# A selective scan whose delta products share TensorE's rows, whose sums are split in two, and whose transposed input is stored once

## The chip, the core and the metric

The kernel runs on one core of a Trainium2 chip. The core has TensorE (PE in the profile; its weight loads are PEld), VectorE (DVE), ScalarE (ACT), GpSimd (POOL) and SyncE (SP), which issues nearly all DMAs of this kernel. Each engine works through its own queue in order and waits on semaphores. The metric is the device time of one execution in microseconds.

## The reference

Four layers follow each other on a tensor of 2 x 128 x 128 pixels with 128 channels, each as `x = x + layer(groupnorm(x))`: window attention, a Fourier layer with a feed-forward part, a recurrence in the Fourier domain, and a selective scan (layer 3). Only layer 3 is touched. Cut to what matters:

```
xc = silu(depthwise_conv3x3(x @ W_in[:, :256]))             # 256 channels
xs = [rows, columns, rows reversed, columns reversed]       # four orders of the pixels, within 4 x 4 blocks of 32 x 32
for k in range(4):
    dt(8), B(16), C(16) = split(x_proj_w[k] @ xs[k])         # per pixel
    delta = softplus(dt_proj_w[k] @ dt + dt_proj_b[k])       # 256 x pixels
    h[d, n] = exp(delta * A[d, n]) * h[d, n] + delta * xs[k][d] * B[n]    # scan over 16384 pixels
    y[k][d] = sum_n h[d, n] * C[n] + D[d] * xs[k][d]
out = (layernorm(sum of the y[k] put back in place) * silu(z)) @ W_out
```

All arithmetic is float32. TensorE works a float32 product off in two passes, which the trace shows as two instructions.

## The kernel before

`layer3_conv` makes `xc` and stores it twice: `xs` (channels on partitions, in two orders of pixels: rows and columns) and `xst` (pixels on partitions, 256 channels each, also in both orders). For one of the 32 blocks (`b`, `hg`, `wg`) it transposes the block on TensorE into `xt`, and SP writes it to `xst[0]` with one DMA (L1242) and to `xst[1]`, in column order, with four DMAs (L1245).

`layer3_scan` has 256 **parts**: 2 images x 4 orders k x 32 stretches of 512 pixels. k = 0 and 1 go forward, k = 2 and 3 backward. A part has 8 **slots**: slot s works on four of the 16 states of one half e of the channels (qq = s // 2, e = s % 2), as four scans over 128 x 512 elements. What one slot needs is made by five engines:

- ACT: `exponentials` (L1517, four activations into `da`), `diagonals` (L1538; small diagonal matrices `dg` with B, 8 or 4 copies in turn), and `kept` (L1601, the last states of the scans);
- PE: two units of `products` (L1567; `ups`, 64 passes each, one unit for each two scans, in two PSUM buffers);
- DVE: four scans (L1589), two after each unit of products;
- POOL: `weighted` (L1608, `hs` times C, one instruction for all four scans of a slot), and in every second slot a fourth of the `dg` tiles (L1532);
- PE: `sums` (L1550, 8 passes, which add the weighted states to `yps`).

The loop over slots g writes the engines' queues by hand (`in_order` keeps each engine to the order of the program). One turn g is: the step "head" of the table `steps`; `exponentials(g + 1)`; `kept(g - 1)`; `diagonals(g + 5)`; `weighted(g - 1)`; `tiles(g)`, which is products of half 0, scan 0, steps "0", scan 1, steps "1", products of half 1, scan 2, steps "2", scan 3, steps "3"; then `sums(g - 2)`; then the steps "end". So `kept(g - 1)` and `weighted(g - 1)` run while slot g is scanned, and the sums of slot g - 2 stand in PE's queue between the second products of slot g and the first of slot g + 1.

The table `steps` places the work that comes once a part (slot numbers within the part; the work is for the next part where it makes inputs, for the part before where it takes results):

- slot 7: `project` e = 0 (L1342) before the second products, e = 1 after them, into the PSUM tile `xdps`;
- slot 0: `projected` (ACT copies `xdps` to `xd`: 8 rows dt, 16 rows B, 16 rows C), then `turn_b` on PE (L1360);
- slot 1: `turned_b` on DVE (L1367, `bt`) behind scan 0; `ranks(0)` on PE (L1374, `dtps`) before the second products and `ranks(1)` after them; behind scan 3 `skip(0)` on DVE (L1444 or L1449), which reads `yps` of e = 0;
- slot 2: `softplus` (ACT L1385, with two loads of activation tables), `spread` (DMAs), and `skip(1)` behind scan 3;
- slot 4: `turn` (L1410, both before the second products); slot 5: `turned` (DVE L1422, `du`, behind scans 0 and 1), and in backward parts `unturn` on PE (L1473, both after the second products); slot 6: in backward parts `store` (ACT L1483) at the head, and `load_u` (L1333, `ut`; in the part from 10000.36 it is issued at 10031.92 us and read at 10073.41 us) at the end.

The tiles of `xdps`, `btps`, `dtps`, `dltps` and `ytps` share two PSUM buffers (tag "misc") in turn: `dtps` of e = 0 takes the buffer of `xdps`, `dtps` of e = 1 that of `btps`, which `turned_b` frees. `yps` has one buffer for each e.

`ranks` takes 65 rows of `xd`: rows 0 to 7 are dt, row 64 is all ones for the bias, and the rows of `dtw` between are zero.

Of the kernel before, what the change touches and what calls it, by code (L numbers as in the profile page):

```python
# [9 lines left out]
F32 = mybir.dt.float32  # L10
# [1109 lines left out]
def layer3_conv(tc, cs, ins, x3, xs, xst, sc, sh):  # L1120
# [11 lines left out]
    with ExitStack() as ctx:  # L1132
# [20 lines left out]
        for b in range(NB):  # L1153
            for hg in range(4):
# [62 lines left out]
                for wg in range(4):  # L1217
                    t = f"{b}_{hg}_{wg}"
                    xv = two.tile([P, 2, 32, 32], F32, name=f"xv_{t}", tag="xv")
                    for e in range(2):  # L1220
                        nc.scalar.copy(xv[:, e], xw[e][:, wg].rearrange("p h w -> p w h"))
                        nc.sync.dma_start(
                            xs[0, b, hg, wg, :, e, :], xw[e][:, wg].rearrange("p h w -> p (h w)")
                        )
                        nc.sync.dma_start(
                            xs[1, b, hg, wg, :, e, :], xv[:, e].rearrange("p w h -> p (w h)")
                        )
                    xt = two.tile([P, 8, 256], F32, name=f"xt_{t}", tag="xt")
                    for g in range(4):
                        tps = ps_t.tile([P, 2, 2, P], F32, name=f"xtps_{t}_{g}", tag="x3t")  # L1230
                        for j in range(2):
                            for e in range(2):
                                h0 = 4 * (2 * g + j)
                                nc.tensor.transpose(
                                    tps[:, j, e, :],
                                    xw[e][:, wg, h0 : h0 + 4, :].rearrange("p h w -> p (h w)"),
                                    cs.ident,
                                )
                        nc.scalar.copy(
                            xt[:, 2 * g : 2 * g + 2, :], tps.rearrange("p j e d -> p j (e d)")  # L1240
                        )
                    nc.sync.dma_start(xst[0, b, hg, wg].rearrange("(t p) d -> p t d", p=P), xt)  # L1242
                    cols = xst[1, b, hg, wg].rearrange("(w t h) d -> h w t d", t=8, h=4)
                    for h in range(4):
                        nc.sync.dma_start(cols[h], xt[32 * h : 32 * h + 32])  # L1245


def layer3_scan(tc, cs, ins, xs, xst, yc, ys):
# [9 lines left out]


    nc = tc.nc  # L1260
    NS, DR, NX, T = 16, 8, 40, 512
    with ExitStack() as ctx:
        pool = lambda name, bufs, **kw: ctx.enter_context(tc.tile_pool(name=name, bufs=bufs, **kw))
        w = pool("l3b_w", 1)
# [8 lines left out]
        sel = w.tile([P, 64], F32, name="sel")  # L1273
        nc.sync.dma_start(sel, ins["c_sel64"])
        xpw = w.tile([P, 4, 2, NX], F32, name="xpw")
        for k in range(4):
            nc.sync.dma_start(xpw[:, k], ins["x_projT"][k].rearrange("(e p) c -> p e c", p=P))

        dtw = w.tile([65, 4, 256], F32, name="dtw")
        nc.sync.dma_start(dtw, ins["dt_ext"])  # L1280
        xds = []
        for i in range(2):
            t = w.tile([65, T], F32, name=f"xd{i}")
            nc.gpsimd.memset(t, 0.0)
            nc.gpsimd.memset(t[64:65, :], 1.0)
            xds.append(t)

        dsk = w.tile([P, 2, 2, 2], F32, name="dsk")
# [22 lines left out]
        def tag_of(i):  # L1311
            return "_".join(map(str, parts[i]))
# [5 lines left out]
        def steps_of(rows, tb):  # L1318
            return rows.rearrange("p (j t) -> p t j", t=4)[:, tb]
# [8 lines left out]
        def load_u(i):  # L1328
            b, k, s, sub = parts[i]
            _, (hg, wg) = place(i)  # L1330
            ut = one.tile([P, 4, 256], F32, name=f"ut_{tag_of(i)}", tag="ut")
            px = xst[k % 2, b, hg, wg]
            nc.sync.dma_start(ut, px.rearrange("(s p m) d -> s p m d", s=2, m=4)[sub])  # L1333
            held[i]["ut"] = ut

        def project(e):
# [11 lines left out]
        def projected(i):  # L1348
            v = held[i]
            xd = xds[i % 2]  # L1350
            nc.scalar.copy(xd[0:NX, :], v["xps"][0:NX, :])
            v["cd"] = dr.tile([NS, T], F32, name=f"cd_{tag_of(i)}", tag="cd")
            nc.sync.dma_start(v["cd"], xd[DR + NS : NX, :])
            v["xd"] = xd

        def turn_b(i):
            v = held[i]
            v["bps"] = ps_m.tile([P, 4, NX], F32, name=f"btps_{tag_of(i)}", tag="misc")
            for j in range(4):
                nc.tensor.transpose(  # L1360
                    v["bps"][:, j, :], steps_of(v["xd"][0:NX, :], j), cs.ident[0:NX, 0:NX]
                )

        def turned_b(i):
            v = held[i]
            v["bt"] = two.tile([P, 4, NX], F32, name=f"bt_{tag_of(i)}", tag="bt")
            nc.vector.tensor_copy(v["bt"], v["bps"])  # L1367

        def ranks(e):
            def f(i):  # L1370
                k = parts[i][1]
                v = held[i]
                ps = ps_m.tile([P, T], F32, name=f"dtps_{tag_of(i)}_{e}", tag="misc")
                nc.tensor.matmul(  # L1374
                    ps, dtw[:, k, e * P : (e + 1) * P], v["xd"], start=True, stop=True
                )
                v.setdefault("dps", []).append(ps)
            return f


        def softplus(i):
            v = held[i]
            dl = one.tile([P, 2, T], F32, name=f"dl_{tag_of(i)}", tag="dl")
            for e in range(2):
                nc.scalar.activation(dl[:, e, :], v["dps"][e], AF.Softplus)  # L1385
            v["dl"] = dl

        def spread(i):
# [88 lines left out]
        def store(i):  # L1477
# [23 lines left out]
        def at(g, place):  # L1501
            for r, where, step in steps:
                i, rest = divmod(g - r, 8)
                if where == place and rest == 0 and 0 <= i < len(parts):
                    step(i)
# [31 lines left out]
                    for n in range(4):  # L1537
                        nc.scalar.activation(dg[:, n, :], sel, AF.Copy, scale=bt[:, n : n + 1])  # L1538

        def sums(g):  # L1540
            i, s, qq, e = slot_of(g)
            v = held[i]
            if qq == 0:
                v.setdefault("yps", {})[e] = ps_y.tile(
                    [P, T], F32, name=f"yps_{tag_of(i)}_{e}", tag=f"yps{e}"
                )
            hs = v.pop(("hs", s))
            for q in range(2):
                for h in range(2):
                    nc.tensor.matmul(  # L1550
                        v["yps"][e][64 * h : 64 * h + 64, :], sel, hs[:, 2 * h + q, :],
                        start=(qq == 0 and q == 0), stop=(qq == 3 and q == 1),
                    )

        def products(g, half):
            i, s, qq, e = slot_of(g)
# [17 lines left out]
        def tiles(g):  # L1574
            i, s, _, _ = slot_of(g)
            b, k, _, _ = parts[i]
            rev = k >= 2
            v = held[i]
            state = states[(b, k)]
            da = v.pop(("da", s))  # L1580
            hs = four.tile([P, 4, T], F32, name=f"hs_{tag_of(i)}_{s}", tag="hs")
            for half in range(2):
                ups = products(g, half)
                for q in range(2):
                    j = 2 * half + q
# [3 lines left out]
                    nc.vector.tensor_tensor_scan(  # L1589
                        o, a, u, state[:, 4 * s + j : 4 * s + j + 1], ALU.mult, ALU.add  # L1590
                    )
                    at(g, j)
            v[("hs", s)] = hs

        def kept(g):
# [17 lines left out]
        with in_order(tc):  # L1613
            for g in range(-13, slots + 7):
                at(g, "head")
                if 0 <= g + 1 < slots:
                    exponentials(g + 1)
                if 0 <= g - 1 < slots:
                    kept(g - 1)
                if 0 <= g + 5 < slots:  # L1620
                    diagonals(g + 5)
                if 0 <= g - 1 < slots:
                    weighted(g - 1)
                if 0 <= g < slots:
# [124 lines left out]
def program(tc, ins, out):  # L1749
    nc = tc.nc  # L1750
    with ExitStack() as ctx:
# [7 lines left out]
        xst = dram.tile([2, NB, 4, 4, 1024, 256], F32, name="xst")  # L1759
# [102 lines left out]
```

## Time and profile before

| | |
|---|---|
| time, median of 3 runs | 18188.72 us (18179.59 to 18199.93) |
| the profiled execution, time / span | 18196.57 us / 18194.8 us |
| mean granted clock of TensorE | 0.95 |
| PE / DVE / ACT / POOL busy | 85% / 82% / 71% / 57% of the span |
| scan stage: first and last scan start | 6328.7 us, 17676.3 us: 256 parts of 44.3 us on average |
| scans, L1589 | 8192, mean 1260 ns, busy 9831.4 us; idle before them 963.1 us |
| weighted, L1608 | 2048, mean 4549 ns |
| products, L1567 | 131072 passes, busy 4488.2 us |
| sums, L1550 | 16384 passes, mean 635 ns, busy 4408.7 us |
| ranks, L1374 | 1024 passes, mean 646 ns, busy 577.7 us |
| column copies of xst, L1245 | 128 DMAs of 256 KB, 582 / 1474 / 2526 ns (least, median, most) on SP |

"Busy" is the time in which at least one instruction of the group runs, so passes that run side by side count once. "Idle before" is the engine's idle time ahead of the group, with the engine and line whose semaphore ended it. PE's instructions overlap by about 0.1 us at their ends. "issue" as the cause of a PEld gap means that no wait of the profile ended it.

### The profile page before, as it was taken

The numbers are of one execution on the slowest core, as the hardware profiler recorded it, in microseconds if no ns is written. First come the engines' busy times: TensorE is split into PE (matmuls) and PEld (weight loads), VectorE is DVE, ScalarE is ACT, GpSimd is POOL, SyncE is SP. The second block draws the span as 40 slices with busy tenths as digits, with TensorE's granted clock in tenths as the row PEclk, the third lists the DMA queues.
The fourth block names the chain that finished last, engine by engine and source line by source line (L and its number), as shares of the span: only waits on it lengthen the run. The fifth ranks groups of instructions, "written<-read, shape, count | busy, mean of one in ns | idle before, by whom it ended". The sixth has DMA issues, their size and how long they took to land.

```text
span 18194.8 us, 466190 instructions
## 1 busy us (share of the span) xinstructions
PE 15391.5 (85%) x196098; PEld 8884.8 (49%) x196098; DVE 14937.3 (82%) x18937; ACT 12999.8 (71%) x29537; POOL 10298.8 (57%) x3930
## 2 busy tenths in 40 slices
PE   7888888888666688888888888888888888888888
PEld 5555555674223344444444444444444444444445
DVE  5766666335997699999899998999999999999986
ACT  4665666333554588888888888888888888888874
POOL 0000000011000088888888888888888888888871
PEclk9999999889888799999999999999999999999999
DMA  2000000121124644444444444444444444444446
GB/s 45 23 24 23 17 17 17 57 72 54 51 57 155 207 107 116 108 118 120 119 115 108 113 117 119 120 112 114 108 113 120 123 117 108 112 112 120 118 127 192
DMA packets 1085881, 1770.68 MB, mean 97 GB/s; under 512 B 108494, under 2 KB 476878, under 8 KB 1081487
## 3 DMA queue, kind: packets, MB, share of 16 engines
q1 hardware_dynamic: 1009918, 1716.69, 35.6%
q8 instruction: 1552, 25.43, 0.6%
q10 hardware_dynamic: 73872, 24.16, 0.5%
q14 instruction: 539, 4.41, 0.1%
HBM read 1128.22 MB, written 343.93 MB: 81 GB/s over the span
## 4 chain that ended last, share of the span: by engine, by line
DVE 25%; ACT 22%; PE 19%; issue 4%; DMA 3%; SPq 1%; POOL 1%; DVEq 0%; ACTq 0%; POOLq 0%
DVE hs L1589 17%; ACT da L1517 9%; PE yps L1550 7%; PE ups L1567 6%; ACT dg L1538 5%; PE xdps L1342 2%; ACT L1385 2%; DVE du L1422 2%; ACT L1517 2%; ACT dl L1385 2%; DVE acc L1208 1%; DMA xc<-xs 1%; DMA cb<-cd 1%; POOL hs L1608 1%; ACT states L1601 1%
## 5 line engine op out<-in xcount | busy, mean ns | idle before, releaser
L1589 DVE TENSOR_TENSOR_SCAN hs<-da,states,ups 128x512 f32<-128x512 f32 x8192 | 9831.4, 1260 | 963.1 <-PE ups L1567 652.9
L1608 POOL TENSOR_TENSOR hs<-hs,cb 128x2048 f32<-128x2048 f32 x2048 | 9295.4, 4549 | 1516.5 <-ACT states L1601 1194.8
L1517 ACT ACTIVATE da<-db,na 128x512 f32<-128x512 f32 x8192 | 5224.3, 710 | 3.1
L1567 PEld LDWEIGHTS ups<-dg,du 64*64 64x64 f32 x131072 | 3611.4, 133 | 3081.9 <-issue 2811.0
L1567 PE MATMUL ups<-dg,du 64*64 64x128 f32 x131072 | 4488.2, 276 | 710.4 <-DVE hs L1589 612.7
L1550 PE MATMUL yps<-hs,sel 128*64 128x512 f32 x16384 | 4408.7, 635 | 378.7 <-POOL hs L1608 375.2
L1538 ACT ACTIVATE dg<-sel,bt 128x64 f32<-128x64 f32 x12288 | 3152.1, 335 | 0.3 <-PE ups L1567 0.2
L1550 PEld LDWEIGHTS yps<-hs,sel 128*64 128x64 f32 x16384 | 1114.1, 141 | 2268.7 <-issue 1787.4
L386 PE MATMUL tps<-ident,s 128*128 128x128 f32 x8192 | 1230.6, 288 | 434.8 <-DVE pT L389 270.2
L391 ACT COPY pT<-tps 128x512 f32<-128x512 f32 x1280 | 722.9, 584 | 1118.9 <-PE tps L386 1118.6
L306 POOL TENSOR_TENSOR xres<-xres,rowb 128x256 f32<-128x256 f32 x128 | 94.2, 737 | 2449.6 <-DMA xres<-in_x 1831.9
L358 DVE CUSTOM_DVE_ANT_1 s<-sps,relbias 128x512 f32<-128x512 f32 x2048 | 1321.0, 682 | 139.8 <-PE sps L341 134.4
L386 PEld LDWEIGHTS tps<-ident,s 128*128 128x128 f32 x8192 | 902.5, 144 | 1029.9 <-issue 499.5
L1601 ACT COPY states<-hs 128x4 f32<-128x4 f32 x2048 | 386.3, 189 | 1407.1 <-DVE hs L1589 1406.8
L371 ACT ACTIVATE s<-s,nm 128x1024 f32<-128x1024 f32 x1024 | 1163.7, 1138 | 130.3 <-DVE nm L369 127.5
L1156 POOL MEMSET xpad<- 128x34 f32 x8 | 1.3, 162 | 1153.0 <-PE xs L1030 1104.7
L1532 POOL TENSOR_TENSOR dg<-sel,bt 128x256 f32<-128x256 f32 x1024 | 633.1, 618 | 7.5 <-DVE bt L1367 7.5
L341 PE MATMUL sps<-kc,qT 32*128 32x512 f32 x4096 | 620.9, 675 | 1.9 <-DVE qT L326 1.2
L1342 PE MATMUL xdps<-xc,xpw 128*40 128x512 f32 x1024 | 541.7, 611 | 43.4 <-DMA xpw<-in_x_projT 26.1
L1374 PE MATMUL dtps<-xd,dtw 65*128 65x512 f32 x1024 | 577.7, 646 | 0.3 <-DVE bt L1367 0.2
L389 DVE COPY pT<-tps 128x512 f32<-128x512 f32 x768 | 527.6, 687 | 57.7 <-PE tps L386 55.9
L404 PE MATMUL ops<-pT,v 128*32 128x128 f32 x16384 | 500.3, 274 | 0.0
(283 smaller groups left out, 14782.3 us busy)
## 6 DMA issues: line engine op xcount, KB each, us to landing
cb<-cd SPq DMA_DIRECT2D x512, 1024.0 KB
db<-dl SPq DMA_DIRECT2D x1024, 256.0 KB
xc<-xs SPq DMA_DIRECT2D x256, 512.0 KB
ut<-xst SPq DMA_DIRECT2D x256, 512.0 KB
yc<-ysb SPq DMA_DIRECT2D x128, 512.0 KB
yf<-yc SPq DMA_DIRECT2D x128, 512.0 KB
ys<-yt SPq DMA_DIRECT2D x128, 512.0 KB
y<-ys SPq DMA_DIRECT2D x128, 512.0 KB
```

The costliest lines, as they stand in the source:

```text
L358: nc.vector.tensor_tensor_reduce(blocks(v["s", qt][:, h, 512 * g : 512 * g + 512]), blocks(v["sps", qt, g][h]), bias[:, h, :, r0 : r0 + WS ...
L371: nc.scalar.activation(s[:, h, :], s[:, h, :], AF.Exp, bias=nm[:, 2, h : h + 1], scale=-1.0, accum_out=v["sums"][:, qt, h : h + 1],)
L386: nc.tensor.transpose(tps[:, j, :], v["s", qt][:, h, k0 : k0 + P], cs.ident)
L391: nc.scalar.copy(dst, tps)
L1342: nc.tensor.matmul(v["xps"][0:NX, :], xpw[:, k, e, :], v["xc"][:, e, :], start=(e == 0), stop=(e == 1),)
L1385: nc.scalar.activation(dl[:, e, :], v["dps"][e], AF.Softplus)
L1517: nc.scalar.activation(da[:, j, :], held[i]["db"][:, e, j // 2, :], AF.Exp, scale=na[:, k, c : c + 1])
L1538: nc.scalar.activation(dg[:, n, :], sel, AF.Copy, scale=bt[:, n : n + 1])
L1550: nc.tensor.matmul(v["yps"][e][64 * h : 64 * h + 64, :], sel, hs[:, 2 * h + q, :], start=(qq == 0 and q == 0), stop=(qq == 3 and q == 1),)
L1567: nc.tensor.matmul(out[64 * n : 64 * n + 64, r, tb], v["du"][64 * r : 64 * r + 64, tb, 64 * row : 64 * row + 64], dg[:, :, n, :], start=Tr ...
L1589: nc.vector.tensor_tensor_scan(o, a, u, state[:, 4 * s + j : 4 * s + j + 1], ALU.mult, ALU.add)
L1608: nc.gpsimd.tensor_tensor(hs, hs, cb.unsqueeze(1).to_broadcast([P, 2, 2 * T]), ALU.mult)
```

## The change

Three edits, all in layer 3:

1. **One copy of `xst`.** `layer3_conv` writes each block once, in row order. `load_u` reads the column orders (k odd) from it with eight DMAs instead of one, each for every eighth partition, in runs of 1 KB where they were 4 KB.
2. **`ranks` in two row groups.** `x_proj` gets zero columns and a second copy of dt, so that `xd` has 56 rows: dt in rows 0 to 7 and again in 32 to 39, B in 8 to 23, C in 40 to 55. The product of e = 0 uses rows 0 to 31, that of e = 1 rows 32 to 63, and both are issued one after the other in slot 1, before the second products. The bias goes into the softplus activation. `xpw`, `dtw` and the new `dtb` are loaded with 12, 2 and 1 DMAs instead of 4 and 1, after two memsets.
3. **`sums` in two halves.** The four passes of q = 0 of `sums(g - 2)` stand behind the first products of slot g (and the steps "0" and "1"), those of q = 1 behind the second products (and the steps "2" and "3").

```diff
-                    nc.sync.dma_start(xst[0, b, hg, wg].rearrange("(t p) d -> p t d", p=P), xt)
-                    cols = xst[1, b, hg, wg].rearrange("(w t h) d -> h w t d", t=8, h=4)
-                    for h in range(4):
-                        nc.sync.dma_start(cols[h], xt[32 * h : 32 * h + 32])
+                    nc.sync.dma_start(xst[b, hg, wg].rearrange("(t p) d -> p t d", p=P), xt)
...
-    NS, DR, NX, T = 16, 8, 40, 512
+    NS, DR, NX, T = 16, 8, 56, 512
...
+        nc.gpsimd.memset(xpw, 0.0)
         for k in range(4):
-            nc.sync.dma_start(xpw[:, k], ins["x_projT"][k].rearrange("(e p) c -> p e c", p=P))
+            xp = ins["x_projT"][k].rearrange("(e p) c -> p e c", p=P)
+            for to, of, n in ((0, 0, DR + NS), (32, 0, DR), (32 + DR, DR + NS, NS)):
+                nc.sync.dma_start(xpw[:, k, :, to : to + n], xp[:, :, of : of + n])
...
-            px = xst[k % 2, b, hg, wg]
-            nc.sync.dma_start(ut, px.rearrange("(s p m) d -> s p m d", s=2, m=4)[sub])
+            px = xst[b, hg, wg]
+            if k % 2:
+                cols = px.rearrange("(h m s c) d -> s h c m d", h=8, m=4, s=2)[sub]
+                for h in range(8):
+                    nc.sync.dma_start(ut[h::8], cols[h])
+            else:
+                nc.sync.dma_start(ut, px.rearrange("(s p m) d -> s p m d", s=2, m=4)[sub])
...
-        def ranks(e):
-            def f(i):
...
-                ps = ps_m.tile([P, T], F32, name=f"dtps_{tag_of(i)}_{e}", tag="misc")
-                nc.tensor.matmul(
-                    ps, dtw[:, k, e * P : (e + 1) * P], v["xd"], start=True, stop=True
-                )
...
+        def ranks(i):
+            k = parts[i][1]
+            v = held[i]
+            v["dps"] = [
+                ps_m.tile([P, T], F32, name=f"dtps_{tag_of(i)}_{e}", tag="misc") for e in range(2)
+            ]
+            for e in range(2):
+                rows = slice(32 * e, 32 * e + 32)
+                nc.tensor.matmul(v["dps"][e], dtw[rows, k, :], v["xd"][rows, :], start=True, stop=True)
...
-                nc.scalar.activation(dl[:, e, :], v["dps"][e], AF.Softplus)
+                nc.scalar.activation(
+                    dl[:, e, :], v["dps"][e], AF.Softplus, bias=dtb[:, k, e : e + 1]
+                )
...
-            (-8, 1, turn_b), (-7, 0, turned_b), (-7, 1, ranks(0)), (-7, 2, ranks(1)),
+            (-8, 1, turn_b), (-7, 0, turned_b), (-7, 1, ranks),
...
-        def sums(g):
+        def sums(g, q):
...
-            hs = v.pop(("hs", s))
-            for q in range(2):
-                for h in range(2):
-                    nc.tensor.matmul(
-                        v["yps"][e][64 * h : 64 * h + 64, :], sel, hs[:, 2 * h + q, :],
-                        start=(qq == 0 and q == 0), stop=(qq == 3 and q == 1),
-                    )
+            hs = v[("hs", s)]
+            for h in range(2):
+                nc.tensor.matmul(
+                    v["yps"][e][64 * h : 64 * h + 64, :], sel, hs[:, 2 * h + q, :],
+                    start=(qq == 0 and q == 0), stop=(qq == 3 and q == 1),
+                )
...
                     at(g, j)
+                if g >= 2:
+                    sums(g - 2, half)
...
-                if 0 <= g - 2 < slots:
-                    sums(g - 2)
```

`turn_b` and `turned_b` move 32 rows instead of 40; the copy of `xdps` to `xd` moves 56 rows instead of 40.

More of the change, by code (lines that the diff above doesn't have):

```diff
@@ L1275, in layer3_scan @@
         xpw = w.tile([P, 4, 2, NX], F32, name="xpw")
+        nc.gpsimd.memset(xpw, 0.0)
         for k in range(4):
-            nc.sync.dma_start(xpw[:, k], ins["x_projT"][k].rearrange("(e p) c -> p e c", p=P))
-        dtw = w.tile([65, 4, 256], F32, name="dtw")
-        nc.sync.dma_start(dtw, ins["dt_ext"])
+            xp = ins["x_projT"][k].rearrange("(e p) c -> p e c", p=P)
+            for to, of, n in ((0, 0, DR + NS), (32, 0, DR), (32 + DR, DR + NS, NS)):
+                nc.sync.dma_start(xpw[:, k, :, to : to + n], xp[:, :, of : of + n])
+        dtw = w.tile([64, 4, P], F32, name="dtw")
+        nc.gpsimd.memset(dtw, 0.0)
+        for e in range(2):
+            nc.sync.dma_start(
+                dtw[32 * e : 32 * e + DR], ins["dt_ext"][0:DR, :, e * P : e * P + P]
+            )
+        dtb = w.tile([P, 4, 2], F32, name="dtb")
+        ext = ins["dt_ext"]
+        nc.sync.dma_start(dtb, bass.AP(ext.tensor, ext.offset + 64 * 1024, [[1, P], [256, 4], [P, 2]]))
         xds = []
         for i in range(2):
-            t = w.tile([65, T], F32, name=f"xd{i}")
+            t = w.tile([64, T], F32, name=f"xd{i}")
             nc.gpsimd.memset(t, 0.0)
-            nc.gpsimd.memset(t[64:65, :], 1.0)
             xds.append(t)
@@ L1352, in projected @@
             v["cd"] = dr.tile([NS, T], F32, name=f"cd_{tag_of(i)}", tag="cd")
-            nc.sync.dma_start(v["cd"], xd[DR + NS : NX, :])
+            nc.sync.dma_start(v["cd"], xd[32 + DR : NX, :])
             v["xd"] = xd
@@ L1357, in turn_b @@
             v = held[i]
-            v["bps"] = ps_m.tile([P, 4, NX], F32, name=f"btps_{tag_of(i)}", tag="misc")
+            v["bps"] = ps_m.tile([P, 4, 32], F32, name=f"btps_{tag_of(i)}", tag="misc")
             for j in range(4):
                 nc.tensor.transpose(
-                    v["bps"][:, j, :], steps_of(v["xd"][0:NX, :], j), cs.ident[0:NX, 0:NX]
+                    v["bps"][:, j, :], steps_of(v["xd"][0:32, :], j), cs.ident[0:32, 0:32]
                 )
@@ L1365, in turned_b @@
             v = held[i]
-            v["bt"] = two.tile([P, 4, NX], F32, name=f"bt_{tag_of(i)}", tag="bt")
+            v["bt"] = two.tile([P, 4, 32], F32, name=f"bt_{tag_of(i)}", tag="bt")
             nc.vector.tensor_copy(v["bt"], v["bps"])
-        def ranks(e):
-            def f(i):
-                k = parts[i][1]
-                v = held[i]
-                ps = ps_m.tile([P, T], F32, name=f"dtps_{tag_of(i)}_{e}", tag="misc")
-                nc.tensor.matmul(
-                    ps, dtw[:, k, e * P : (e + 1) * P], v["xd"], start=True, stop=True
-                )
-                v.setdefault("dps", []).append(ps)
-            return f
+        def ranks(i):
[4 more added lines that the diff above has]
+            ]
+            for e in range(2):
+                rows = slice(32 * e, 32 * e + 32)
+                nc.tensor.matmul(v["dps"][e], dtw[rows, k, :], v["xd"][rows, :], start=True, stop=True)
         def softplus(i):
             v = held[i]
+            k = parts[i][1]
             dl = one.tile([P, 2, T], F32, name=f"dl_{tag_of(i)}", tag="dl")
             for e in range(2):
-                nc.scalar.activation(dl[:, e, :], v["dps"][e], AF.Softplus)
+                nc.scalar.activation(
+                    dl[:, e, :], v["dps"][e], AF.Softplus, bias=dtb[:, k, e : e + 1]
+                )
             v["dl"] = dl
@@ L1538, in diagonals @@
                         nc.scalar.activation(dg[:, n, :], sel, AF.Copy, scale=bt[:, n : n + 1])
-        def sums(g):
+        def sums(g, q):
             i, s, qq, e = slot_of(g)
             v = held[i]
-            if qq == 0:
+            if qq == 0 and q == 0:
                 v.setdefault("yps", {})[e] = ps_y.tile(
@@ L1546, in sums @@
                 )
-            hs = v.pop(("hs", s))
-            for q in range(2):
-                for h in range(2):
-                    nc.tensor.matmul(
-                        v["yps"][e][64 * h : 64 * h + 64, :], sel, hs[:, 2 * h + q, :],
-                        start=(qq == 0 and q == 0), stop=(qq == 3 and q == 1),
-                    )
+            hs = v[("hs", s)]
[3 more added lines that the diff above has]
+                    start=(qq == 0 and q == 0), stop=(qq == 3 and q == 1),
+                )
+            if q == 1:
+                del v[("hs", s)]
         def products(g, half):
@@ L1628, in layer3_scan @@
                         at(g, j)
-                if 0 <= g - 2 < slots:
-                    sums(g - 2)
+                    for q in range(2):
+                        if 0 <= g - 2 < slots:
+                            sums(g - 2, q)
                 at(g, "end")
@@ L1758, in program @@
         xs = dram.tile([2, NB, 4, 4, P, 2, 1024], F32, name="xs")
-        xst = dram.tile([2, NB, 4, 4, 1024, 256], F32, name="xst")
+        xst = dram.tile([NB, 4, 4, 1024, 256], F32, name="xst")
         yc = dram.tile([NB, 2, 16, 2, P, 2, 512], F32, name="yc")
```

## The prediction

> **What bounds the kernel now.** I read the busy time by stage first, then the waits of the scan stage, then the timelines of one part, last the chain through the convolution stage.
>
> ```profile
> core 0: us, PE busy (x) PEld busy (x) DVE busy (x) ACT busy (x) POOL busy (x), PEclk, DMA share, GB/s
> 5629.00:6284.00 655.00, 443.44 (x1308) 216.19 (x1306) 457.59 (x380) 340.19 (x398) 4.17 (x37) 0.83 0.68 217
> 9500.00:10500.00 1000.00, 883.58 (x13662) 477.78 (x13656) 932.67 (x850) 839.36 (x2130) 881.73 (x277) 0.97 0.44 110
> ```
>
> The second row is a piece of the scan stage (11,349 us of 18,195): DVE 93%, but PE, POOL and ACT 84 to 88%. No engine is free, and buffers are short, so the order of the queues decides. The first row is `layer3_conv`: no engine above 70%, DMA 0.68.
>
> ```profile
> POOL hs L1608 <- ACT states L1601: 1194.8, 694, 32.1
> DVE hs L1589 <- PE ups L1567: 652.9, 822, 22.3
> PE yps L1550 <- POOL hs L1608: 372.5, 291, 2.4
> ```
>
> DVE loses most to products that come late (653 us), and PE loses time in front of sums, because POOL has not finished weighting. Below, P is a unit of products, S a slot's sums, W a `weighted`, and (1,0) means slot 1, half 0. I count t from the first scan of the part at 10045.96 us; the next part's is at 10088.27, so it takes 42.31 us. PE in slots 1 and 3, then DVE:
>
> ```profile
> 10049.23 1.10 PE L1567 MATMUL ups<-dg,du 64*64 64x128 f32 x32
> 10050.26 1.12 PE L1374 MATMUL dtps<-xd,dtw 65*128 65x512 f32 x2
> 10051.32 1.10 PE L1567 MATMUL ups<-dg,du 64*64 64x128 f32 x32
> 10052.35 1.12 PE L1374 MATMUL dtps<-xd,dtw 65*128 65x512 f32 x2
> 10053.41 1.94 PE L1550 MATMUL yps<-hs,sel 128*64 128x512 f32 x8
> 10055.27 1.98 PE L1567 MATMUL ups<-dg,du 64*64 64x128 f32 x64
> ...
> 10061.48 1.10 PE L1567 MATMUL ups<-dg,du 64*64 64x128 f32 x32 [1.24 <-DVE hs L1589]
> 10063.98 1.94 PE L1550 MATMUL yps<-hs,sel 128*64 128x512 f32 x8 [1.39 <-POOL hs L1608]
> ```
> ```profile
> 10051.84 0.30 DVE L1367 COPY bt<-btps 128x160 f32<-128x160 f32 x1
> 10052.06 3.62 DVE L1589 TENSOR_TENSOR_SCAN hs<-da,states,ups 128x512 f32<-128x512 f32 x3
> 10055.59 0.72 DVE L1444 SCALAR_TENSOR_TENSOR ysb<-xc,dsk,yps 128x512 f32<-128x512 f32 x1
> 10056.54 4.79 DVE L1589 TENSOR_TENSOR_SCAN hs<-da,states,ups 128x512 f32<-128x512 f32 x4 [0.23 <-PE ups L1567]
> ```
>
> From these starts: a P holds PE 1.04, `ranks` of one e 1.06, S 1.87 (half an S: 0.93 and a second change of shape, 1.01); scans follow each other every 1.17; from the start of P to its first scan 1.27; PE starts 0.15 after the scan that frees `ups`. Note that P(1,1) at 10051.32 goes *before* `ranks(1)`, which needs `bt`'s buffer, free only at 10052.14; and that P(3,1) goes before the S that waits for POOL.
>
> **Part by part: the queue of PE in the scan stage.** I replay one forward part in the new order with these durations.
>
> Slot 0: P(0,0), `turn_b`, half S, P(0,1): P(0,1) starts at 1.38 instead of 0.36, its scans at 2.65 instead of 2.37. First scan of slot 1: 4.99 (4.71).
>
> Slot 1: `bt` ends at 6.46. The product of e = 0 has its buffer; that of e = 1 waits for `bt`, now in front of everything else: queued behind it are half S, P(1,1), half S, P(2,0). It starts at 6.52. How long do two row groups take?
>
> ```profile
> 804.68 1.14 PE L341 MATMUL sps<-kc,qT 32*128 32x512 f32 x8
> ```
>
> Four products of the same shape in layer 0, eight passes in 1.14 us: they do run side by side, so `ranks` would cost 1.06 once instead of twice. But the wait decides: `ranks` ends at 7.58, half S at 8.59, P(1,1) feeds scan 2 at 9.86. DVE would be ready at 7.55: it stands 2.3 us. First scan of slot 2: 12.84, before 10.58. The 1.06 us that PE saves lies inside this wait and is worth nothing here.
>
> Slots 2 and 3: half S of the next part's slot 0 must wait for `skip` to read `yps` (12.92), which was no matter before; it ends at 13.99 and P(2,1) is in time. ACT's softplus and exponentials end as before, so W of slot 1 ends at 18.34 (17.96 before, 10063.92). The half S that waits for it stands in front of P(3,1): scan 2 of slot 3 at 20.69, 0.1 late. Slot 4 starts at 23.03, before at 21.16: of 2.3 + 0.3 us lost, the old waits ahead of slots 2 and 4 (0.23 and 0.44) absorb 0.7.
>
> Slots 4 to 7: W of slot 2 ends at 22.88, `turn` holds PE to 23.67, half S to 24.68: scans late by 0.55. Slots 5 and 6: none. Slot 7: 0.24 behind W of slot 5 (39.16). Behind the second `project` the last half S is only 1.0 long, so P of the next part feeds its scan at 44.42; before, the stall there was 0.69, now 0.58. The part takes **44.42 us, 2.11 more**. The same replay of the old order gives each scan of this part within 0.1 us. A backward part has `unturn`; its first P of slot 6 comes sooner (stall 2.1 us now, 0.66 then), but `store` delays `kept`, W of slot 5 ends at 40.45 and scan 2 of slot 7 stands 0.87: 45.70 against 43.6, again 2.1. Times 256: **+540 us**.
>
> **The clock.** Not all parts take 42.3 or 43.6 us. By the first scans of all parts, forward ones average 43.88 and backward ones 44.81; undisturbed ones are 1.57 and 1.21 faster. The reason, in the part before:
>
> ```profile
> 10015.20:10018.60 3.40, 1.32 (x34) 1.09 (x36) 3.40 (x4) 3.40 (x12) 3.40 (x2) 0.99 0.99 221
> 10018.60:10022.00 3.40, 3.40 (x12) 0.61 (x12) 2.49 (x3) 3.40 (x10) 3.40 (x1) 0.50 1.08 249
> ```
>
> When PE is busy for less than about 1.6 us of a stretch of 3.4 us, its granted clock is 0.50 in the next: the sums there take 3.56 us instead of 1.94. The old order makes two gaps side by side in slot 3 (1.24 and 1.39 above). In the replay the longest gaps are about 1.6 (slot 1), 1.3 and 1.3 (slots 2 and 3), each alone within 3.4 us, so PE stays at 1.8 us or more. I let a third of the excess remain: 1.39 x 256 x 2/3 = **-237 us**; bounds 0 and -356.
>
> [...]
>
> **One copy of xst.** Between two groups of rows the chain through `layer3_conv` is SP and DMA; some of its pieces:
>
> ```profile
> 5795.99 1.40 SPq L1245
> 5797.43 1.95 SPq L1245
> 5799.42 6.03 DMA xst<-xt
> 5805.55 1.08 ACT xt L1239 x2
> ```
>
> On the chain from 5620 to 6340 us L1245 has 11.0%, 79 us, and the transfers of xst 6.2%, 45 us. Both can go, but ACT's copies (25 us in each 61 us gap of DVE) stand behind them. I take **-75**, bounds -40 and -110. In the scan, seven more issues in 128 parts, 0.3 to 0.6 us each on SP (rows of L1333 and L1397), with `ut` issued 41 us before its use and SP idle between: nothing; without that cover, 4 us x 128 = 512. The start of the stage issues 10 more loads of about 0.46 us ahead of `na`, which is on the chain: **+5**. The softplus bias and the narrower `bt` (0.30 to about 0.25): nothing.
>
> **Sum.** 18,196.6 + 540 - 237 - 75 + 5 = 18,430. The profiled execution is 8 us above the median, so 18,422.
>
> **Rivals.**
> - *The clock stays as disturbed as before* (the gaps fall together after all): 18,196.6 + 540 - 75 + 5 - 8 = 18,659. For it: PE's total idle time hardly changes. Against: the replay spreads it.
> - *No half-clock stretch is left, and the convolution gains its most*: 540 - 356 - 110 + 5, so 18,268. For it: no replayed stretch is under 1.8 us.
> - *The products do not run side by side* (the second pass of e = 0 also waits behind `bt` and the second product comes after it): 1.06 more in slot 1, nothing behind it to absorb it: +271, 18,693. Against: the row of L341.
> - *Faster:* P of the next slot stands behind a half S instead of a whole one, so DVE's waits for `ups` shrink. At most all 653 us go, with 75 of the convolution 17,461; half of them, 17,790. It decides if W ends before P(g,0) is done and `bt` is ready when PE reaches `ranks`. The third row of waits and the replay speak against both: PE reaches `ranks` at 4.5, `bt` ends at 6.5.
>
> **How the numbers follow.** Forecast 0.52; clock as before 0.16; no half clock 0.14; not side by side 0.08; faster 0.10. The replay is off by perhaps 0.4 us a part, 100 us. A measurement tells 0.2%, 36 us, from no change; the case without half clock comes that near in about a third. Faster 0.10, same 0.05, slower 0.85. The range goes from the third case less part of that error, 18,230, to the fourth, 18,700.
>
> **What would show it.** DVE's wait for `ups` grows, mostly ahead of scan 2 of slot 1 (about 2.3 us, 256 times), and PE waits about 1.6 us for `bt` in L1374. The busy time of L1374's successor halves. PE waits for POOL oftener, and half-clock stretches become rare. The column issues are gone from the chain of `layer3_conv`, and the first scan starts about 70 us earlier. I am wrong if scan 2 of slot 1 does not wait, or if parts get shorter than 43.6 us.

## The result, and the profile after

| | before | after |
|---|---|---|
| median of 4 runs | 18185.44 us | 18518.22 us |
| ratio, with its 95% interval | | 1.0181 [1.0164, 1.0199] |
| the profiled execution, time / span | 18196.57 / 18194.8 us | 18519.72 / 18517.9 us |
| first scan, last scan start | 6328.7, 17676.3 us | 6168.9, 17996.5 us |
| scan stage between them | 11347.5 us | 11827.6 us |
| an undisturbed forward / backward part | 42.31 / 43.61 us | 44.50 / 45.72 us |
| mean forward / backward part | 43.88 / 44.81 us | 45.64 / 46.83 us |
| starts of a half-clock stretch in the scan stage | 168 | 162 |

("Undisturbed" is the 5th percentile of the parts, taken from the first scans of all 256.) The change makes the kernel 1.8% slower. The 323 us between the two profiled executions are a first scan that comes 160 us earlier, a scan stage that takes 480 us more, and 3 us elsewhere.

The busy time by stage in after: a piece of `layer3_conv` that ends 45 us ahead of the first scan, as the row of before did, and the same piece of the scan stage.

```profile
5629.00:6124.00 495.00, 424.73 (x1316) 198.04 (x1314) 458.88 (x383) 339.99 (x403) 4.16 (x37) 0.95 0.62 224
9500.00:10500.00 1000.00, 880.15 (x13048) 443.06 (x13048) 897.80 (x810) 809.19 (x2032) 841.00 (x262) 0.97 0.44 106
```

The convolution does the same work (DVE 459 us, ACT 340 us) in 495 us instead of 655, and its granted clock is 0.95 instead of 0.83. In the scan stage DVE goes from 93% to 90% and POOL from 88% to 84%, at the same clock of 0.97: the engines wait more, for each other.

The waits of after:

```profile
POOL hs L1624 <- ACT states L1617: 1281.9, 664, 38.9
DVE hs L1603 <- PE ups L1581: 1065.0, 1317, 25.8
PE yps L1562 <- POOL hs L1624: 408.2, 635, 3.2
PE dtps L1388 <- DVE bt L1378: 255.0, 255, 1.5
```

DVE's wait for products grew from 653 to 1065 us, PE's waits for weighted states came 635 times instead of 291, and the last line is new: once a part, PE waits for `bt`. PE in slots 1 to 3 of an undisturbed part (its first scan is at 10043.21 us), then DVE in slot 1:

```profile
10047.66 1.12 PE L1388 MATMUL dtps<-xd,dtw 32*128 32x512 f32 x2
10049.77 1.09 PE L1388 MATMUL dtps<-xd,dtw 32*128 32x512 f32 x2 [0.99 <-DVE bt L1378]
10050.79 1.08 PE L1562 MATMUL yps<-hs,sel 128*64 128x512 f32 x4
10051.80 1.10 PE L1581 MATMUL ups<-dg,du 64*64 64x128 f32 x32
...
10056.28 1.08 PE L1562 MATMUL yps<-hs,sel 128*64 128x512 f32 x4 [1.33 <-DVE ysb L1457]
...
10061.77 1.08 PE L1562 MATMUL yps<-hs,sel 128*64 128x512 f32 x4 [1.33 <-POOL hs L1624]
10062.78 1.10 PE L1581 MATMUL ups<-dg,du 64*64 64x128 f32 x32
```
```profile
10049.36 0.26 DVE L1378 COPY bt<-btps 128x128 f32<-128x128 f32 x1
10053.04 2.45 DVE L1603 TENSOR_TENSOR_SCAN hs<-da,states,ups 128x512 f32<-128x512 f32 x2 [2.23 <-ACT dl L1396]
```

The first line is the product of e = 0, both passes; the second is that of e = 1, 2.1 us later, behind `bt`. The two don't run side by side. Behind them stand a half S and P(1,1), and DVE waits 2.23 us for scan 2 of slot 1. The profile names ACT's softplus there, which ended 0.03 us before the scan began; but P(1,1), which the scan reads, had started 1.24 us before it, about the usual distance (1.27 in the part of before). Further down, the half S of slot 1 waits for POOL in front of P(3,1).

Fold all parts: ahead of scan 2 of slot 1 DVE stands 3.04 us on average in forward parts (3.16 in backward ones), and 0.5 us ahead of scan 2 of slot 4. And 159 of the 162 starts of a half-clock stretch now lie in slot 1, where before had none (there they lay in slots 3 and 5 or 6).

### The profile page after: what moved, and what is told of

Same layout as the page of the kernel before. It is cut to its first block, busy times and chain, and to the rows that moved or that the text cites. A ratio compares the mean times of both kernels' runs of the same rounds, so it can differ in the third digit from the quotient of the medians.

```text
span 18517.9 us, 467052 instructions
## 1 busy us (share of the span) xinstructions
PE 15768.0 (85%) x196098; PEld 8713.8 (47%) x196098; DVE 15016.5 (81%) x18937; ACT 13109.7 (71%) x29538; POOL 10305.6 (56%) x3930
## 4 chain that ended last, share of the span: by engine, by line
DVE 29%; PE 28%; ACT 11%; issue 5%; DMA 2%; POOL 1%; SPq 1%; DVEq 0%; POOLq 0%; ACTq 0%
DVE hs L1603 21%; PE ups L1581 11%; PE yps L1562 10%; ACT dg L1551 3%; ACT da L1530 3%; PE dltps L1423 1%; PE xdps L1353 1%; DMA cb<-cd 1%; ACT L1396 1%; ACT dl L1396 1%; DVE du L1435 1%; POOL hs L1624 1%; PE btps L1371 1%; DVE acc L1208 1%; PE dtps L1388 1%
## 5 line engine op out<-in xcount | busy, mean ns | idle before, releaser
L1603 DVE TENSOR_TENSOR_SCAN hs<-da,states,ups 128x512 f32<-128x512 f32 x8192 | 9943.1, 1264 | 1364.9 <-PE ups L1581 1065.0
L1562 PE MATMUL yps<-hs,sel 128*64 128x512 f32 x16384 | 4779.2, 634 | 904.9 <-POOL hs L1624 408.2
L1581 PEld LDWEIGHTS ups<-dg,du 64*64 64x64 f32 x131072 | 3670.3, 136 | 3603.8 <-issue 3120.1
L1581 PE MATMUL ups<-dg,du 64*64 64x128 f32 x131072 | 4689.9, 281 | 122.3 <-DVE hs L1603 71.4
L1562 PEld LDWEIGHTS yps<-hs,sel 128*64 128x64 f32 x16384 | 910.7, 137 | 2080.0 <-issue 1236.8
L1388 PE MATMUL dtps<-xd,dtw 32*128 32x512 f32 x1024 | 584.7, 651 | 255.5 <-DVE bt L1378 255.0
L1353 PE MATMUL xdps<-xc,xpw 128*56 128x512 f32 x1024 | 548.4, 618 | 34.6 <-DMA xc<-xs 20.8
```

Source lines behind the costliest of these rows:

```text
L1353: nc.tensor.matmul(v["xps"][0:NX, :], xpw[:, k, e, :], v["xc"][:, e, :], start=(e == 0), stop=(e == 1),)
L1388: nc.tensor.matmul(v["dps"][e], dtw[rows, k, :], v["xd"][rows, :], start=True, stop=True)
L1562: nc.tensor.matmul(v["yps"][e][64 * h : 64 * h + 64, :], sel, hs[:, 2 * h + q, :], start=(qq == 0 and q == 0), stop=(qq == 3 and q == 1),)
L1581: nc.tensor.matmul(out[64 * n : 64 * n + 64, r, tb], v["du"][64 * r : 64 * r + 64, tb, 64 * row : 64 * row + 64], dg[:, :, n, :], start=Tr ...
L1603: nc.vector.tensor_tensor_scan(o, a, u, state[:, 4 * s + j : 4 * s + j + 1], ALU.mult, ALU.add)
```

## Experiments

Two readings of the longer part stood against each other. **A**, the prediction's: the wait for `bt` in front of P(1,1) decides. **B**: the earlier due time decides, because half an S now stands in front of the second products, where POOL has not finished W. For the clock, **C**: what counts is how many rows of the array a pass fills, so that passes of 32 rows hardly count as work; **D**: the idle gap alone.

All differences below are against the kernel before, run on the same chip.

| run | median us | ratio [95%] | scan stage us | undisturbed part, forward / backward | half-clock starts |
|---|---|---|---|---|---|
| e1_copy | 18022.14 | 0.9912 [0.9897, 0.9927] | 11343.2 | 42.31 / 43.62 | 152 |
| e2_ranks | 18552.46 | 1.0209 [1.0193, 1.0225] | 11704.6 | 42.52 / 43.81 | 272 |
| e3_split | 18525.28 | 1.0192 [1.0177, 1.0207] | 11694.0 | 44.25 / 45.55 | 115 |
| e4_late | 18895.65 | 1.0394 [1.0377, 1.0412] | 12214.6 | 46.55 / 47.79 | 252 |
| e8_order | 18243.42 | 1.0032 [1.002, 1.0044] | 11411.2 | 42.37 / 43.62 | 136 |
| e5_rows65 | 18394.33 | 1.0111 [1.0096, 1.0126] | 11725.2 | 44.54 / 45.71 | 86 |
| e9_rows128 | 18286.35 | 1.0053 [1.0038, 1.0068] | 11599.2 | 44.53 / 45.71 | 3 |
| e6_whole | 18075.82 | 0.9939 [0.9923, 0.9956] | 11407.7 | 42.52 / 43.81 | 184 |
| e7_later | 17480.90 | 0.9611 [0.9597, 0.9626] | 10805.0 | 41.60 / 42.49 | 8 |
| e10_both | 17808.96 | 0.9795 [0.9779, 0.9811] | 11122.1 | 41.78 / 42.69 | 172 |

**e1_copy: edit 1 alone.**

```diff
 # before, plus (cut)
-                    cols = xst[1, b, hg, wg].rearrange("(w t h) d -> h w t d", t=8, h=4)
-                    for h in range(4):
-                        nc.sync.dma_start(cols[h], xt[32 * h : 32 * h + 32])
+                for h in range(8):
+                    nc.sync.dma_start(ut[h::8], cols[h])
```

> The kernel before with the first edit alone (one copy of xst). In the changed kernel the first scan starts at 6168.9 us instead of 6328.7, 160 us earlier. If the copies alone do that, and the eight loads of ut cost nothing in the scan: 160 us faster than before, about 18,025, with parts of 42.3 and 43.6 us where undisturbed. If the loads of ut cost time in the scan stage, the stage gets longer than 11,348 us and the gain is smaller, down to none at 0.6 us a part. If the earlier start comes from the other edits' loads, the time stays at 18,185.

It gains 162 us, as expected. The first scan comes 171 us earlier, and the scan stage is 4 us shorter than before: the seven additional DMAs in 128 parts cost nothing. (The date of the first scan varies by itself: before and e3, which are alike up to it, have 6328.7 and 6308.7 us, so the 160 us of after and the 171 of e1 are not told apart.) Where the gain lies, by the group of DVE in `layer3_conv`, first of before, then of e1:

```profile
L1208 DVE SCALAR_TENSOR_TENSOR acc<-xz,cv,cps 128x1024 f32<-128x1024 f32 x64 | 81.4, 1275 | 159.3 <-ACT xz L1190 122.9 <-PE cps L1199 18.7 <-ACT xw L1212 17.7
```
```profile
L1208 DVE SCALAR_TENSOR_TENSOR acc<-xz,cv,cps 128x1024 f32<-128x1024 f32 x64 | 81.7, 1277 | 19.5 <-PE cps L1199 14.5 <-ACT xw L1212 4.8
```

The two gaps of 61 us between groups of rows (122.9 us) vanish whole.

**e2_ranks: edit 2 alone.**

```diff
 # before, plus the new x_proj, dtw, dtb and softplus bias (cut)
-            (-8, 1, turn_b), (-7, 0, turned_b), (-7, 1, ranks(0)), (-7, 2, ranks(1)),
+            (-8, 1, turn_b), (-7, 0, turned_b), (-7, 1, ranks),
```

> The kernel before with the second edit alone (ranks of both e in 32-row groups before the second products, sums whole). By my replay the wait for bt costs 1.3 us in slot 1 (scan 2 at 8.6 instead of 7.3), of which the old waits ahead of slots 2 and 4 absorb most: undisturbed forward parts of 42.7 us instead of 42.3, about 100 us in all, 18,290; with half-clock stretches in slot 1 as in the changed kernel up to 18,450. If the wait for bt is what costs the changed kernel its time (theory A), nothing absorbs it: 256 times 2.3 us, 18,700 or more (the changed kernel without its gain in the convolution).

**e3_split: edit 3 alone.**

```diff
 # before, plus (cut)
+                if g >= 2:
+                    sums(g - 2, half)      # behind the products of this half
```

> The kernel before with the third edit alone (sums in two halves, ranks as before). Theory B, by the replay: the half of the sums that waits for POOL stands half a slot earlier, in front of P(3,1), and W of slot 1 ends at about 18.3 us of the part whatever slot 1 does; so scan 2 of slot 3 starts at 20.7 as in the changed kernel and undisturbed forward parts take 44.4 us: 18,186 + 540 = 18,730, and up to 18,950 because PE stands 3.5 us ahead of that half and its clock will be halved in many parts. Theory A (the wait for bt is the cost): ranks(1) no longer stands in front of P(1,1); parts stay near 42.5 to 43 us, 18,200 to 18,350.

e3 alone lengthens the undisturbed part by 1.94 us, nearly all of what the three edits do together (2.15). DVE's long wait is then not in slot 1 (0.45 us) but ahead of scan 2 of slot 3: 1.94 us on average in forward parts, 2.27 in backward ones. PE's waits for weighted states in e3 (before: 372.5 us in 291 waits):

```profile
PE yps L1549 <- POOL hs L1611: 1097.9, 1047, 4.1
```

e2 alone lengthens the undisturbed part by only 0.2: DVE stands 1.5 us in slot 1, on average, but makes it good in the slots behind. What e2 costs is clock: 272 starts of half-clock stretches, 131 of them in slot 1, and its mean part is 2.6 us above the undisturbed one (before: 1.39). Neither time was expected: e2 lies above its 18,450 us because of the clock, and e3 below the 18,730 of theory B, since half clock became rarer there (115 starts, a mean part 0.8 us above the undisturbed one) where it was to become more frequent.

The scan stage is 357 us longer in e2 and 347 in e3, but only 480 in after. The undisturbed parts do add up (0.2 and 1.94, against 2.15 together). What doesn't is the clock: by the distance of the mean part from the undisturbed one, times 256 and against before, it costs about 305 us in e2 and gives back 150 in e3 and 66 in after.

**e4_late: after, with `ranks` behind the second products, so that nothing waits for `bt`.**

```diff
-            (-8, 1, turn_b), (-7, 0, turned_b), (-7, 1, ranks),
+            (-8, 1, turn_b), (-7, 0, turned_b), (-7, 2, ranks),
```

> The changed kernel with both ranks behind the second products of slot 1 instead of before them, so that bt is ready when PE reaches them. Theory A (the wait for bt in front of P(1,1) is the cost): 2.1 to 2.3 us a part come back, about 17,950. Theory B (the half of the sums that waits for POOL in front of P(3,1) is the cost): the wait in slot 1 goes, a wait of the same size appears at scan 2 of slot 3, undisturbed forward parts still take 44.4 us, 18,500, and up to 18,750 with more half-clock stretches. In both the two products run side by side, 1.1 us for four passes; if they do not, 2.1 us.

This is the run that tells A from B. Under A the 2.2 us come back; measured, the kernel is 2.1% slower than after, by the two ratios. B has the place of the wait, but not the time: it allowed up to 18,750 us. PE in slots 1 to 3 of the corresponding part:

```profile
10177.17 1.13 PE L1388 MATMUL dtps<-xd,dtw 32*128 32x512 f32 x4
...
10183.67 1.10 PE L1581 MATMUL ups<-dg,du 64*64 64x128 f32 x32
10188.27 1.97 PE L1562 MATMUL yps<-hs,sel 128*64 128x512 f32 x4 [3.50 <-POOL hs L1624]
10190.17 1.99 PE L1581 MATMUL ups<-dg,du 64*64 64x128 f32 x32
```

Both products now find their buffers free, so the four passes run side by side, in 1.13 us, and P(1,1) is on time. But the half S of slot 1 waits 3.50 us for POOL, and behind it stands P(3,1). Behind that gap half S and P take 1.97 and 1.99 us instead of 1.08 and 1.10; half clock starts 252 times in the 256 parts. The 46.55 us in the table are therefore of disturbed parts; the three forward parts without half clock take 44.9. Mean wait of DVE ahead of scan 2 of slot 3: 3.89 us in forward parts.

Why is W so late when scan 2 of slot 1 is early? In POOL's queue W of slot 1 is released by `kept` (10183.38 to 10183.56; W starts at 10183.69). `kept` stands on ACT behind softplus, its two loads of tables (1.28 us each) and four exponentials (10176.54 to 10183.47), and softplus starts only when `ranks` is done. So here the date of W hangs not on the scans, the last of which ended at 10179.83, but on ACT; the half S was put in front of that date.

**e8_order: before, with `ranks(1)` in front of P(1,1), 65 rows as before.**

```diff
-            (-8, 1, turn_b), (-7, 0, turned_b), (-7, 1, ranks(0)), (-7, 2, ranks(1)),
+            (-8, 1, turn_b), (-7, 0, turned_b), (-7, 1, ranks(0)), (-7, 1, ranks(1)),
```

> The kernel before with ranks(1) moved in front of the second products of slot 1, next to ranks(0): products of 65 rows, sums whole, two copies of xst. It differs from the run with the second edit alone (18,552 us) only in the rows that the products use (65 against 32) and in the loads and the bias. In that run undisturbed parts take 42.5 and 43.8 us, 0.2 more than before, but 131 half-clock stretches begin in slot 1, where the kernel before has none. Theory C (products of 32 rows count for less than their time in what the clock is granted for): none begin in slot 1 here, parts average 44.2 and 45.0, 18,200 to 18,300. Theory D (the idle time ahead of the product that waits for bt is what halves the clock): they begin here just as often, 18,500 to 18,600.

The wait for `bt` alone, with whole sums: the undisturbed part is 42.37 us, 0.06 more than before, and 0.3% on the time. By itself the wait that the prediction held decisive is worth next to nothing. Against e2, which has the same order with 32 rows, slot 1 has 17 half-clock starts instead of 131; theory C had forecast none.

**e5_rows65 and e9_rows128: after, with `ranks` of 65 rows as before, and of 128 rows (zeros below the 65).** Order and waits are those of after. The cut shows the product alone; e5 and e9 also have the old `x_proj`, `xd` and `bt` of 40 columns and the bias in row 64, so it is e5 and e9 that differ in nothing but the rows.

```diff
 # e5, against after (cut)
-                nc.tensor.matmul(v["dps"][e], dtw[rows, k, :], v["xd"][rows, :], start=True, stop=True)
+                nc.tensor.matmul(ps, dtw[:, k, e * P : (e + 1) * P], v["xd"], start=True, stop=True)
 # e9, against e5
-        dtw = w.tile([65, 4, 256], F32, name="dtw")
+        dtw = w.tile([P, 4, 256], F32, name="dtw")     # and xd of 128 rows
```

> The changed kernel with the products of ranks in the old form of 65 rows, both in front of the second products of slot 1 as in the changed kernel; one copy of xst and split sums stay. The replay gives the same 44.4 us for an undisturbed forward part. Theory C: the half-clock stretches that begin in slot 1 in 159 parts of the changed kernel are gone, parts average 44.6 to 44.8 and 45.8 to 46.0, 18,280 to 18,350. Theory D: they stay, 18,519.

> As the changed kernel with products of 65 rows (18,394 us), but the two products of ranks read 128 rows, of which the added 63 are zero on both sides: same results, same durations, same waits. In the traces so far every stretch of 3.41 us whose busy time, weighted by active rows / 128, is under about 0.42 is followed by half clock, and none above 0.45; unweighted, the changed kernel's are at 0.65 and overlap with undisturbed ones. If the rows count (theory C): the 85 half-clock stretches that begin in slot 1 with 65 rows (159 with 32) fall to nearly none, parts average 44.6 and 46.0, 18,250 to 18,310. If they do not: 18,394.

All three have the same undisturbed part (44.50, 44.54, 44.53 us), and half-clock starts in slot 1 of 159, 85 and 0. The time falls by 232 us from after to e9 by their medians, 108 of them from e5 to e9, although the passes work on more rows. e5 lies between the two forecasts: theory C had expected that 65 rows are enough. Two successive stretches of 3.41 us, with their granted clock in the column ahead of the last two; first of after, then of e9:

```profile
10182.70:10186.12 3.42, 2.42 (x35) 1.26 (x32) 3.42 (x5) 2.86 (x11) 3.42 (x2) 1.00 0.02 5
10186.12:10189.53 3.41, 3.41 (x14) 0.72 (x16) 0.59 (x1) 3.36 (x5) 3.41 (x2) 0.50 0.00 0
```
```profile
10009.35:10012.76 3.41, 2.38 (x36) 1.17 (x28) 3.41 (x5) 2.84 (x11) 3.41 (x2) 1.00 0.00 0
10012.76:10016.18 3.42, 3.42 (x42) 1.26 (x40) 1.18 (x2) 3.37 (x5) 3.42 (x2) 1.00 0.02 5
```

Both begin 3.6 to 3.7 us behind a part's first scan and hold the same passes in the same order: PE is busy for 2.42 and 2.38 us, with a gap of 1.0 us in each. Behind the first stretch the granted clock is 0.50, behind the second 1.00. The passes of `ranks` have 32 rows in the one and 128 in the other. So D fails in these runs, and C holds, though not as sharply as it was told: with 65 rows the starts in slot 1 are about half as many (85 for 159), with 128 rows there are none.

**e6_whole: edits 1 and 2, sums whole, `ranks` side by side behind P(1,1).**

```diff
 # before, plus edits 1 and 2 (cut), and
+            (-8, 1, turn_b), (-7, 0, turned_b), (-7, 2, ranks),
```

> The first and second edits without the third: one copy of xst, ranks side by side but behind the second products of slot 1, sums whole behind them as before. By theory B and the replay nothing waits for bt or earlier for POOL than in the kernel before; PE saves 1.06 us a part in slot 1, and W of slot 1 (13.4 to 18.0 us) ends when it did, so the saving is given back in slot 3: 18,022 as with the first edit alone, within 40. If the saving is worth something: down to 17,750. If 32-row products halve the clock also where they stand between other work: 18,100 to 18,300.

18,076 us, beside 18,022 for e1: the intervals just overlap. The pair behind P(1,1) gains nothing here; if anything it costs, since the scan stage is 64 us longer than in e1, with 184 half-clock starts instead of 152.

**e7_later: edit 1, and the sums split like in edit 3 but half a slot later; `ranks` as before.**

```diff
 # before, plus edit 1 and (cut)
+                if half == 0 and g >= 3:
+                    sums(g - 3, 1)
+                if half == 1 and g >= 2:
+                    sums(g - 2, 0)
```

> One copy of xst, ranks as in the kernel before, and the sums in two halves that come half a slot later instead of half a slot earlier: q = 0 of slot g - 2 behind the second products of slot g, q = 1 of slot g - 3 behind the first. The burst is split as in the changed kernel, but no half has to wait for POOL earlier than the whole sums did. Theory B: the cost of the split lies in the earlier deadline, so this one costs nothing: undisturbed forward parts 42.1 to 42.5 us, backward ones up to 0.9 shorter than 43.6 because the products of slot 6 stand behind half a burst; 17,850 to 18,050. If the split costs by its additional changes between products and sums (0.15 us each, two a slot): 2.4 us a part, 18,500 to 18,650.

17,481 us: 3.9% faster than before and, by the two ratios, 5.6% faster than after. The expectation had the sign, but not the size: it did not foresee that the half clock goes away too, 8 starts instead of 168. The same group of scans as above, and PE in slots 2 and 3:

```profile
L1592 DVE TENSOR_TENSOR_SCAN hs<-da,states,ups 128x512 f32<-128x512 f32 x8192 | 9854.6, 1262 | 397.9 <-PE ups L1570 225.5 <-ACT da L1519 106.3 <-POOL dg L1534 2.9
```
```profile
9700.24 1.10 PE L1570 MATMUL ups<-dg,du 64*64 64x128 f32 x32
9702.74 1.08 PE L1551 MATMUL yps<-hs,sel 128*64 128x512 f32 x4 [1.40 <-POOL hs L1615]
9703.75 1.10 PE L1570 MATMUL ups<-dg,du 64*64 64x128 f32 x32
```

P(3,1) (first line) now stands in front of the half S that waits for POOL. That wait is still there, 1.40 us, but what it delays is P(4,0), for which DVE has no need yet. DVE's waits for products fall from 653 us (before) and 1065 (after) to 226. As the sums are split here too, the additional changes of shape between products and sums can't be what made e3 slower. Against e1, from which e7 differs in the sums alone, it gains 541 us: about 235 by shorter undisturbed parts, the rest by the clock.

**e10_both: e7 with edit 2, `ranks` side by side behind P(1,1).**

```diff
 # e7, plus edit 2 (cut), and
-            (-8, 1, turn_b), (-7, 0, turned_b), (-7, 1, ranks(0)), (-7, 2, ranks(1)),
+            (-8, 1, turn_b), (-7, 0, turned_b), (-7, 2, ranks),
```

> The run with later halves of the sums (17,481 us) plus the second edit with both ranks behind the second products of slot 1, side by side. By the replay PE has that time to spare there: the waits of DVE that it can shorten (scan 2 of slot 1 0.12, slot 2 0.04) are worth 0.16 us a part, 40 us, 17,440. If the 32-row products push stretches under the clock's threshold: each costs up to 1.7 us, 17,500 to 17,700. If the pair is worth its 1.06 us a part: 17,210.

It misses its expectation by far: 328 us slower than e7. The undisturbed part is only 0.2 us longer; there are 172 half-clock starts instead of 8, 164 of them in slot 3. Rows of `ranks` are not the reason: none of the stretches ahead of these 164 starts holds a pass of `ranks`, and PE is busy in them for 0.35 to 0.46 of the time. PE's waits for POOL in e7, then in e10, and the stretch ahead of one start:

```profile
PE yps L1551 <- POOL hs L1615: 378.3, 345, 2.5
PE yps L1562 <- POOL hs L1626: 511.3, 286, 2.7
```
```profile
11645.36:11648.77 3.41, 1.41 (x20) 0.42 (x16) 3.41 (x4) 3.41 (x13) 3.41 (x2) 1.00 0.90 287
```

In that stretch PE stands 2.00 us in front of a half S (1.40 at the same place in the part of e7 above). The author's guess is that the time saved by the pair in slot 1 (in e4 its four passes took 1.13 us) becomes idle time in front of POOL, and idle time half clock; a run that fills the saved time again, which would show it, was not made.

## Why the prediction was right in sign and near in size, and where it was not

**The sign and the sum.** Forecast +233 us on the profiled execution, measured +323. The sum is nearer than its terms by luck: the clock gave back 171 us less than forecast, the convolution with the start 90 us more, and the two errors cancel in part. By the terms:

| term | forecast | measured |
|---|---|---|
| undisturbed part, 256 times | +540 (44.42, 45.70) | +550 (44.50, 45.72) |
| half clock | -237 | -66 (the excess falls from 1.39 to 1.13 us a part) |
| convolution and start | -75 and +5 | -160 |

**The replay of PE's queue held**, nearly start by start: scan 2 of slot 1 at 9.86 us (measured 9.83), of slot 3 at 20.69 (20.80), the end at 44.42 (44.52 in this part). Three of its signs came as told: DVE's wait for `ups` grows mostly ahead of scan 2 of slot 1, PE waits for POOL oftener, `bt` ends a wait of PE in each part (of 1.0 us, not 1.6). Two did not: the busy time of `ranks` did not halve, and half-clock stretches did not become rare (162 starts after 168).

**The cause given with it was wrong in two places.** First, "But the wait decides": of the two waits the replay put the 2.3 us on that for `bt`, and saw the one in front of P(3,1) as "0.1 late". It has both, so its length of the part came out right; but it did not ask what would be late if the first were not. e8 has the first alone (+0.06 us a part), e3 the second alone (+1.94), e4 takes the first away and loses time. The split's due time is what costs, and e7, with the same split half a slot later, shows it from the other side. Second, `ranks` was to cost 1.06 us once instead of twice and to end at 7.58. In fact the passes of e = 0 ran alone from 4.45, those of e = 1 from 6.56 to 7.65. The rival "not side by side" thus came true in its first half, but its price (+271) did not: it supposed that a pass of e = 0 also waits. The busy time of `ranks` went from 577.7 to 584.7 us; in e4, with both buffers free, it halved (290.5).

**The clock is the term that failed.** The step is "When PE is busy for less than about 1.6 us of a stretch of 3.4 us", with "so PE stays at 1.8 us or more". After has 2.42 us of busy time in such a stretch, 0.71 of it, and still falls to 0.50. In the scan stage of before the 1.6 us fits most stretches: 142 of the 168 starts follow one in which PE is busy for less, and 22 others below it are followed by none. That figure was read without regard to rows. To count them, weight each moment of busy time with the rows of all passes that run in it, at most 128, over 128. By this working from the trace, the stretches of after that precede a half-clock start have a share of 0.47 at most, and 99 in 100 of the others 0.52 or more; unweighted most of the former have 0.71, and over 400 of the others have no more. (The expectation of e9 has 0.65 for these, and 0.42 and 0.45 for the weighted share; by the busy time of the row above, 2.42 of 3.42 us, it is 0.71. If the last 0.12 us of each pass is left out, 0.66 and at most 0.45 come out in before and after, but 15 stretches of before below 0.42 are followed by no start.) With rows counted, 1.6 us in 3.4, a share of 0.47, parts the two kinds in after. The replay's gaps in slots 2 and 3 did become harmless, as it said (3 starts left there and behind); the wait for `bt` with passes of 32 rows put 159 into slot 1. So the outcome is that of the rival "the clock stays as disturbed as before", but not by its reason, gaps that fall together. Its 18,659 lies 141 us above the median, mainly because it has 90 us less for the convolution and the start, and not the 66 us that the clock did win.

**The convolution.** -75 was chosen inside bounds of -40 and -110, and e1 measured -171 for the first scan. The two gaps of DVE, 122.9 us, went whole, so the step that held ACT's copies in them to be next in line was wrong. The rest of the gain may be the granted clock there (0.83 in before, 0.95 in after); no run separates it.

**As told:** the DMAs of `ut` cost nothing (the scan stage of e1 takes 11,343 us, that of before 11,348), and `ranks` side by side gain nothing (e6, 11,408 us).

## What to carry to other kernels

When a step is moved forward in a queue written by hand, ask first what date its input really has, and which engine sets it; a step with a late input belongs behind the work that others wait for, and splitting it paid here only where the pieces stood there (e3 against e7: 1,044 us, of which edit 1, that only e7 has, is worth 162). When a replay shows two waits, price each with the other gone, since removing the first may only uncover the second. Before packing small products into fewer rows, or saving time on PE, look at the granted clock around them: the scan stage had 162 half-clock starts with `ranks` of 32 rows and 3 with 128 (after and e9), and 172 instead of 8 with the pair behind P(1,1) (e10 and e7).

## What was not expected of the hardware

**Half clock came oftener with fewer rows.** In the scan stage of after the granted clock falls to 0.50 for 3.413 us at a time (139 of the 162 starts) or for twice that (23). With the same waits, slot 1 has 159, 85 and 0 starts with passes of `ranks` of 32, 65 and 128 rows. The weighted share above is the author's working from the traces; how the chip counts is not shown. By it, in the twelve traces some 1,700 stretches are followed by a start; 50 of them have a share above 0.50, and only 5 stretches below 0.45 are followed by none. Between 0.45 and 0.50 both kinds occur. The rows of zeros that e9 adds to e5 are worth 108 us, and from after to e9 the time falls by 232 us, about 1.5 us for each start that is gone (232 over 159).

**The packed products ran side by side only where both were ready.** With the buffer of the second not free, the first ran alone for 1.12 us and the second for 1.09 (after); with both free all four passes took 1.13 us (e4).
